# A change at two seams of an FNO, convolution and column-recurrence kernel: where the tile pools lie, the order and queue of the last stores, and who normalises the first columns

## The chip, the cores and the metric

The kernel runs on one core of one Trainium2 chip, as a single program. The metric is its time on the device in microseconds (us), the median over several executions; smaller is better. "The profile" is one further execution, recorded by the hardware profiler: it gives the start and duration of the instructions on each engine, what each waited for, and the traffic of the DMA queues. In its lines PE is TensorE (matmul), DVE VectorE, ACT ScalarE, POOL GpSimd and SP SyncE, which only issues DMAs here. "L733" is line 733 of the kernel before.

## What is computed

The input x has 8 images of 32 channels and 256 x 256 points, in float32. It goes through four layers, each with a group norm (16 groups of two channels) ahead of it and a residual sum behind it:

```python
# layer 0: 32 x 32 modes at either end of the rows are mixed over channels
x = x + _L0_conv_ref(_gn(x), w1r, w1i, w2r, w2i, bias)   # rfft2, einsum, irfft2
# layer 1: the same 5 x 5 kernel on every channel, padding 2
x = x + _L1_conv_ref(_gn(x), kernel, 1, 2)
# layer 2: a gated cell that walks over the columns
x = x + _L2_conv_ref(_gn(x), weight_ih, bias_ih, weight_hh, bias_hh)
# layer 3: running maxima in four directions, then a 1 x 1 convolution
x = x + _L3_conv_ref(_gn(x), W, b)

def _cell(prev_col, cur_col, weight_ih, bias_ih, weight_hh, bias_hh):
    C = cur_col.shape[-1]
    pad = jnp.pad(prev_col, ((0, 0), (1, 1), (0, 0)))
    x = jnp.concatenate([pad[:, :-2], pad[:, 1:-1], pad[:, 2:]], axis=-1)
    i_vals = jnp.einsum('bhk,ok->bho', x, weight_ih) + bias_ih
    h_vals = jnp.einsum('bhc,oc->bho', cur_col, weight_hh) + bias_hh
    ...
    r = jax.nn.sigmoid(r_i + r_h)
    z = jax.nn.sigmoid(z_i + z_h)
    n = jnp.tanh(n_i + r * n_h)
    return n * z + cur_col * (1.0 - z)
```

In layer 2 the first column of the image is the first state; every later column needs the new column to its left and its own normalised values. This makes 255 dependent steps.

## The kernel before

The kernel has four stages, one after another, joined by scratch tensors in DRAM.

**Forward transform and mixing** (`forward_and_mix`, L75). The wanted modes are computed with matmuls and mixed over channels; the mixed modes go from the tiles `sm` to the DRAM tensor `smd`, through the DMA queues of SP and ACT.

**Inverse transform and 5 x 5 convolution** (`inverse_and_conv`, L297). The work runs over 16 units: image b and half h of its channels. Each unit has two parts `ch` of 8 channels. A unit loads its piece of the input into the six buffers `xb` (L379, on GpSimd's DMA queue), and the spectra of its image into `spec` (`load_spectrum`: one DMA of 8-KB rows, two of rows of 128 bytes; the first two images on SP's queue, later ones on ACT's). TensorE forms the inverse transform and the convolution; VectorE adds the residuals (L520) and leaves x1, the input of layer 2, in one of five buffers of 18 KB per partition. The image's 256 columns lie on the partitions in blocks of 28, with 9 tiles for the blocks (`NT = 9`; the last block has tile 0). `squares2` (L525, on ScalarE) takes the sums for the next group norm.

`store(u, ch)` (L534) writes a finished x1 to the DRAM tensor `x2d`, laid out by column: for each quarter `a` of the image's rows it issues three DMAs, the middle blocks, the head (columns 0 to 29, from the tile of block 1) and the tail (the last block). All go through SP's queue; only in the very last store do the odd quarters go through ScalarE's. Behind that store stands the stage's last statement, a fence. In front of it are `statistics(15)` (four small matmuls, four VectorE operations and a `pow` on GpSimd, L569) and `keep` (L572), which puts the last statistics into `stb`.

Columns 0 to 7 of the first seven images are fetched for the recurrence while the last unit is still computed, into the tile `first` (on GpSimd's queue, at the end of the loop over units).

**Column recurrence** (`recurrence`, L684). `turned` (L707) is the transpose of the statistics; from it comes `shift` (L711), the additive term of the normalisation. Eight tiles `hs`, two halves of the batch times four, hold the last states, with one border column at each side of the 64 points; all of every tile is set to zero (L715). Blocks of 8 columns are loaded as `xw` through SP's queue, one DMA for each image (`load`, L720); block 0 is `first`, whose eighth image is loaded here. `normalise` (L731) is one ScalarE operation over 4 columns of one image: tile `xn`. Before the first column all 16 of block 0 are issued.

A step (L807) is one column for one half of the batch (x = 0 or 1); n = 2w + x counts them. In each, the order on the engines is written out by hand:

- TensorE: the matmuls of the gates r, z and n on the old state (`gates`, L786), with the products of the next half step's own column mixed in (`own`, L777).
- ScalarE: sigmoid of r (L828), twice of z (L830 and the next), tanh (L835), then the `normalise` for the next block.
- VectorE: `n = (nh + b) * r` (L829), plus `ni` (L834), then one "piece" of side work (such as the running maximum, L864), times z (L840), plus `a` (L842, the new state in `hs`).
- GpSimd: `a = (1 - z) * x` (L837) and the residual sum of the column (L843), which reads the new state.

ScalarE's sigmoid belongs to another table of functions than the ones that it used before; the load of it stands as ACT_TABLE_LOAD ahead of the first sigmoid.

**Maxima and 1 x 1 convolution** (`maxima_and_mix`, L909).

Inside a stage the order of the instructions on each engine is the order of the program (`manual_schedule`). Each stage opens its own SBUF pools with a `with` block, and they lie one behind another in the order in which they are opened. In `inverse_and_conv` they are, at L314 to L318:

```python
one = ctx.enter_context(tc.tile_pool(name="a2c", bufs=1))   # bias, junk, junk2, five x1
xp = ctx.enter_context(tc.tile_pool(name="a2x", bufs=1))    # spec, xb
wk = ctx.enter_context(tc.tile_pool(name="a2w", bufs=2))    # tt
sm = ctx.enter_context(tc.tile_pool(name="a2s", bufs=3))
```

and in `recurrence` in the same way `one` (turned, shift, hs, bst), `blk` (xw, xn and the running maxima fm), `wk`. The memory of a closed pool is used again by the stage that follows, and the framework adds the waits which that needs. `stb` and `first` have a pool of their own, open over both stages.

Of the kernel before, what the change touches and what calls it, by code (L numbers as in the profile page):

```python
# [10 lines left out]
AF = mybir.ActivationFunctionType  # L11
ALU = mybir.AluOpType
# [5 lines left out]
B, C, H, W = 8, 32, 256, 256  # L18
# [5 lines left out]
A = 4  # L24
Q = H // A


NT = 9
TS = 28
# [263 lines left out]
def columns(x2d, b, lo, hi):  # L293
    return x2d[b, lo:hi].rearrange("w a c q -> (a c) w q")


def inverse_and_conv(tc, k, d, smd, xmean, x2d, stb, first):  # L297
# [6 lines left out]
    nc = tc.nc  # L304
# [6 lines left out]

    PLACES = (1, 2, 3, 5, 6, 7, 8)
    with ExitStack() as ctx:
        one = ctx.enter_context(tc.tile_pool(name="a2c", bufs=1))  # L314
        xp = ctx.enter_context(tc.tile_pool(name="a2x", bufs=1))
        wk = ctx.enter_context(tc.tile_pool(name="a2w", bufs=2))
        sm = ctx.enter_context(tc.tile_pool(name="a2s", bufs=3))
        ps = ctx.enter_context(tc.tile_pool(name="a2p", bufs=1, space=PSUM))  # L318

# [2 lines left out]
        junk = one.tile([P, 16, Q], F32, name="junk")  # L322
# [112 lines left out]
        def squares(u, ch, n, lo, hi, vector=False):  # L435

            for g in range(G):
                x, total = pair_of(u, ch, g, lo, hi), state[u]["sq"][:, ch, g, n : n + 1]
                if vector:
                    nc.vector.scalar_tensor_tensor(  # L440
                        junk2[:, : 2 * (hi - lo)], x, 1.0, x, ALU.mult, ALU.mult, accum_out=total
                    )
                else:
                    nc.scalar.activation(junk[:, : 2 * (hi - lo)], x, AF.Square, accum_out=total)
# [89 lines left out]
        def store(u, ch):  # L534
            b, h = units[u]
            c0 = 2 * CH * h + CH * ch
            x1, to = x1_of(u, ch), x2d[b, :, :, c0 : c0 + CH].rearrange("w a c q -> w a (c q)")
            for a in range(A):
                r = 32 * a
                queue = nc.scalar if a % 2 and 2 * u + ch == 2 * n - 1 else nc.sync  # L540
                queue.dma_start(
                    out=to[TS + 2 : TS * (NT - 1) + 2, a].rearrange("(t w) n -> w t n", w=TS),
                    in_=x1[r + 2 : r + 30, 2:NT].rearrange("w t c q -> w t (c q)"),
                )
                queue.dma_start(out=to[0 : TS + 2, a], in_=x1[r : r + 30, 1].rearrange("w c q -> w (c q)"))
                queue.dma_start(
                    out=to[TS * (NT - 1) + 2 : W, a], in_=x1[r + 2 : r + 32, 0].rearrange("w c q -> w (c q)")
                )

        def statistics(u):  # L550
            b, h = units[u]
# [20 lines left out]
        def keep(u, st):  # L572
            b, h = units[u]
            for kind in range(2):
                nc.vector.tensor_copy(
                    by_pair(stb[:, kind, b, 2 * CH * h : 2 * CH * (h + 1)]), twice(st[:, kind], 2)
                )
# [15 lines left out]
        with tc.manual_schedule(engines=None):  # L593
            load_spectrum(0)
            load_spectrum(1)
            for i in range(3):
                load(0, i)
            spectrum(0)
            for u in range(2):
                begin(u)  # L600
            for c in range(0, CH, 2):
                over_rows(0, c, *(("st", 1), ("up", 3))[c // 2 % 2])
            for p in range(NT):
                transform(0, p)
                if p % 2:
                    over_rows(1, p - 1)
                if p == 4:
                    for ch in range(2):
                        squares(0, ch, 1, 1, 5)
            for ch in range(2):  # L610
                squares(0, ch, 2, 5, NT, ch == 1)
            scale(0, 1, 3)
            transform(1, 0)
            for u in range(n):
                more, beyond = u + 1 < n, u + 2 < n
                for g in range(2 * G):
                    between = []
                    if g == 0 and u == 0:
                        between.append(lambda: scale(u, 0, 3))
                    if g == 3 and more:  # L620
                        between.append(lambda: transform(u + 1, 4))
                    conv(u, g // G, g % G, between)
                    if g < len(PLACES) and more:
                        transform(u + 1, PLACES[g])
                    if g == 2 * G - 1 and beyond:
                        transform(u + 2, 0)
                    if g == 2 * G - 1 and more:
                        scale(u + 1, 0, 3)
                    if g == 1 and u > 0:
                        scale(u, 1)  # L630
                    if g == 2:
                        if u > 0:
                            st = statistics(u - 1)
                        elif beyond:
                            spectrum(units[u + 2][0])
                    if g == G - 1 and beyond:
                        begin(u + 2)
                    if G - 1 <= g < 2 * G - 1 and beyond:
                        over_rows(u + 2, 2 * (g - G + 1))
                    if g == 6 and more:  # L640
                        squares(u + 1, 0, 2, 8, NT)
                    squares2(u, g // G, g % G)
                    if g == 1 and more:
                        for ch in range(2):
                            squares(u + 1, ch, 0, 0, 1)
                    if g == 3 and u > 0:
                        keep(u - 1, st)
                    if g == 5 and more:
                        squares(u + 1, 0, 1, 1, 8)
                    if u % 2 and u + 3 < n:  # L650
                        if g == 2:
                            load_spectrum(units[u + 3][0])
                        elif g == 7:
                            spectrum(units[u + 3][0])
                    if g % G == G - 1 and (u, g) != (n - 1, 2 * G - 1):
                        store(u, g // G)
                    if u == n - 1 and g == G:
                        for b in range(B - 1):
                            nc.gpsimd.dma_start(out=first[:, b], in_=columns(x2d, b, 0, 8))
                if more:  # L660
                    squares(u + 1, 1, 1, 1, NT)
            keep(n - 1, statistics(n - 1))
            store(n - 1, 1)
            tc.declare_fence(nc.tensor.drain().ins, group="conv")

# [18 lines left out]
def recurrence(tc, k, d, x2d, x3d, fwd, stb, first, loaded, mean1, mv3):  # L684
# [10 lines left out]
    with ExitStack() as ctx:  # L695
# [16 lines left out]

        hs = [[one.tile([P, BC, Q + 2], F32, name=f"hs_{x}_{i}") for i in range(NH)] for x in range(NC)]
        for t in hs[0] + hs[1]:
            nc.vector.memset(t, 0.0)  # L715
        bst = one.tile([P, B, NB, 6], F32, name="bst")

        raws, norms, psums = {}, {}, {}
# [1 line left out]
        def load(bi):  # L720
            if bi:
                t = blk.tile([P, B, WB, Q], F32, name=f"xw_{bi}", tag="xw", bufs=4)
                for b in range(B):
                    nc.sync.dma_start(out=t[:, b], in_=columns(x2d, b, bi * WB, (bi + 1) * WB))
            else:
                t = first
                nc.sync.dma_start(out=t[:, B - 1], in_=columns(x2d, B - 1, 0, 8))
            raws[bi] = t
            norms[bi] = blk.tile([P, B, WB, Q], F32, name=f"xn_{bi}", tag="xn")

        def normalise(bi, b, half):  # L731
            w = slice(half * WB // 2, (half + 1) * WB // 2)
            nc.scalar.activation(  # L733
                norms[bi][:, b, w], raws[bi][:, b, w], AF.Identity, bias=shift[:, b : b + 1], scale=sc[:, 1, b : b + 1]
            )
# [142 lines left out]
        with tc.manual_schedule(engines=None):  # L878
            load(0)
            load(1)  # L880
            for half in range(2):
                for b in range(B):
                    normalise(0, b, half)
            for bi in range(NB):
                for wi in range(WB):
                    if wi == WB // 2 and bi + 2 < NB:
                        load(bi + 2)
                    for x in range(NC):
                        step(bi * WB + wi, x)
                        if bi + 1 < NB:  # L890
                            half, b = divmod(NC * wi + x, B)
                            normalise(bi + 1, b, half)
                    running(bi, wi)
                finish(bi)
            tc.declare_fence(nc.tensor.drain().ins, group="signals")
            for piece in pieces[0] + pieces[1]:
                piece()
# [302 lines left out]
```

## Time and profile before

The median of 3 runs is 3101.18 us (3096.61 to 3104.53). The profiled execution took 3099.62 us, of which its span, the time from the first instruction to the last, is 3097.8 us.

Busy time of the engines by stage, in us, as the trace gives it for six windows of the span (PEclk is the granted TensorE clock as a share of full speed; DMA the mean busy share of the 16 DMA engines):

| window | what runs there | length | PE | VectorE | ScalarE | GpSimd | PEclk | DMA |
|---|---|---|---|---|---|---|---|---|
| 0 to 300 | forward, mixing | 300 | 246.4 | 164.5 | 106.6 | 28.9 | 0.85 | 0.86 |
| 300 to 325 | first seam | 25 | 2.0 | 1.7 | 0.0 | 3.3 | 0.50 | 0.99 |
| 325 to 1053 | inverse, convolution | 728 | 705.1 | 557.4 | 481.3 | 117.1 | 0.99 | 0.68 |
| 1053 to 1081 | second seam | 28 | 10.4 | 7.4 | 14.0 | 3.7 | 0.63 | 0.88 |
| 1081 to 2433 | recurrence | 1352 | 1346.0 | 1222.2 | 1111.8 | 700.1 | 1.00 | 0.61 |
| 2433 to 3098 | maxima, 1 x 1 | 665 | 518.1 | 631.1 | 154.9 | 6.8 | 0.90 | 0.82 |
| all | | 3098 | 2827.9 | 2584.2 | 1868.6 | 859.9 | 0.95 | |

A row is read against its length: where an engine's busy time comes near it, that engine has no slack there. In the two seams no compute engine is near its window, and the DMA engines are busy. The granted clock over the whole span is 0.954. Among the largest single groups of instructions of the recurrence, the normalisation (xn from xw) has 496 instructions of 586 ns on ScalarE, and the sum of L843 496 of 685 ns on GpSimd.

### The profile page before, as it was taken

To read this page: it belongs to the slowest core of one execution; us is meant where nothing else is said; L and a number is where in the kernel's file an instruction comes from. 1 tells how busy PE (TensorE), PEld (TensorE's weight loads), DVE (VectorE), ACT (ScalarE), POOL (GpSimd) and SP (SyncE) were. 2 spreads that over 40 slices of the span, in tenths; PEclk is the share of its full clock that TensorE was granted. 3 is DMA by queue.
4 is the path that set the end of the run, shared out by engine and by line. 5 is a ranking of instruction groups with operands and counts; after the bars stand their busy time and mean duration, and the time that the engine had idled before them with its cause. 6 is when DMAs were issued, how large, how long until landed. Compare 5 with 4: busy or idle time off the path is not lost.

```text
span 3097.8 us, 111686 instructions
## 1 busy us (share of the span) xinstructions
PE 2827.9 (91%) x47736; PEld 1625.9 (52%) x47736; DVE 2584.2 (83%) x5178; ACT 1868.6 (60%) x4482; POOL 859.9 (28%) x1247
## 2 busy tenths in 40 slices
PE   7986799999999699999999999999999588888887
PEld 4656244444444366666666666666666333333333
DVE  5753577777777589999999999999999799999997
ACT  3332376667667678888888888888888222222222
POOL 0110011111111255555555555555555300000000
PEclk9985899999999899999999999999999799998998
DMA  9976577777775736656666656666664688888885
GB/s 385 389 278 210 161 226 213 211 210 219 210 215 175 179 91 160 165 143 143 143 150 165 161 142 143 144 155 165 152 146 115 192 319 328 330 322 328 326 327 228
DMA packets 468193, 655.69 MB, mean 212 GB/s; under 512 B 328784, under 2 KB 329696, under 8 KB 441456
## 3 DMA queue, kind: packets, MB, share of 16 engines
q1 hardware_dynamic: 407528, 487.89, 54.1%
q0 software_dynamic: 16784, 84.11, 8.2%
q10 hardware_dynamic: 43384, 76.55, 6.9%
q8 instruction: 374, 6.13, 0.8%
q14 instruction: 123, 1.01, 0.1%
HBM read 371.63 MB, written 272.63 MB: 208 GB/s over the span
## 4 chain that ended last, share of the span: by engine, by line
PE 71%; DVE 20%; DMA 3%; issue 3%; ACT 1%; SPq 0%; POOL 0%; ACTq 0%; DVEq 0%; POOLq 0%
PE vp L487 14%; PE r L753 14%; PE z L753 13%; PE ni L753 6%; PE nh L753 6%; PE up L418 4%; DVE rv L1012 4%; PE yp L131 3%; DVE dq L1018 2%; DVE uq L1020 2%; DVE m L1026 2%; DVE m L1022 2%; DVE m L1024 2%; PE tp L401 2%; PE o L1043 2%
## 5 line engine op out<-in xcount | busy, mean ns | idle before, releaser
L761 PE MATMUL z<-hs,weights 64*64 64x256 f32 x4080 | 539.3, 382 | 0.0
L761 PE MATMUL r<-hs,weights 64*64 64x256 f32 x4080 | 525.0, 375 | 0.0
L761 PE MATMUL ni<-hs,weights 64*64 64x256 f32 x4080 | 524.9, 375 | 0.0
L843 POOL TENSOR_TENSOR xw<-xw,hs 128x256 f32<-128x256 f32 x496 | 339.5, 685 | 635.6 <-DVE hs L842 635.6
L487 PE MATMUL vp<-x,c_conv 64*64 64x512 f32 (+5 forms) x4608 | 460.6, 495 | 4.3 <-DVE x L520 4.3
L1058 ACT ACTIVATE ot<-o,bres 128x512 f32<-128x512 f32 x256 | 154.9, 688 | 505.4 <-PE o L1043 490.0
L520 DVE SCALAR_TENSOR_TENSOR x<-vp,r,x 128x128 f32<-128x128 f32 (+2 forms) x640 | 350.4, 562 | 125.6 <-PE vp L487 106.7
L837 POOL TENSOR_TENSOR a<-zm,xn 128x256 f32<-128x256 f32 x510 | 372.4, 730 | 6.3 <-ACT zm L830 6.1
L835 ACT ACTIVATE n<-n,bih 128x256 f32<-128x256 f32 x510 | 259.2, 508 | 186.3 <-DVE n L834 186.3
L1043 PE MATMUL o<-m,wsc 32*32 32x512 f32 x3072 | 228.6, 724 | 108.1 <-DVE m L1026 104.5
L753 PE MATMUL r<-hs,weights 64*64 64x256 f32 x2040 | 319.1, 389 | 5.0 <-DVE hs L842 4.1
L487 PEld LDWEIGHTS vp<-x,c_conv 64*64 64x64 f32 x4608 | 201.9, 133 | 227.7 <-issue 107.1
L753 PE MATMUL z<-xn,weights 64*64 64x256 f32 x2040 | 305.5, 376 | 14.4 <-ACT xn L733 14.4
L753 PE MATMUL r<-xn,weights 64*64 64x256 f32 x2040 | 305.5, 376 | 1.2 <-ACT rs L828 1.2
L753 PE MATMUL nh<-xn,weights 64*64 64x256 f32 x2040 | 305.7, 377 | 0.0
L753 PE MATMUL z<-hs,weights 64*64 64x256 f32 x2040 | 305.2, 376 | 0.0
L753 PE MATMUL ni<-hs,weights 64*64 64x256 f32 x2040 | 305.2, 376 | 0.0
L733 ACT ACTIVATE xn<-xw,shift,turned 128x256 f32<-128x256 f32 x496 | 290.6, 586 | 0.0
L761 PEld LDWEIGHTS ni<-hs,weights 64*64 64x64 f32 x4080 | 284.5, 133 | 0.3
L829 DVE SCALAR_TENSOR_TENSOR n<-nh,bhh,rs 128x256 f32<-128x256 f32 x510 | 246.3, 483 | 45.9 <-ACT rs L828 31.4
L761 PEld LDWEIGHTS r<-hs,weights 64*64 64x64 f32 x4080 | 280.9, 131 | 0.2
L828 ACT ACTIVATE rs<-r,brz 128x256 f32<-128x256 f32 x510 | 241.3, 473 | 53.9 <-PE r L761 32.5
(162 smaller groups left out, 6233.8 us busy)
## 6 DMA issues: line engine op xcount, KB each, us to landing
xb<-in_xl_dram POOLq DMA_DIRECT2D x96, 768.0 KB, 6.3
xa<-in_xt_dram SPq DMA_DIRECT2D x64, 1024.0 KB
x<-x3d SPq DMA_DIRECT2D x32, 2048.0 KB
fw<-fwd SPq DMA_DIRECT2D x32, 2048.0 KB
out_dram<-ot ACTq DMA_DIRECT2D x64, 1024.0 KB
xw<-x2d SPq DMA_DIRECT2D x248, 256.0 KB
fwd<-fm SPq DMA_DIRECT2D x248, 256.0 KB
x3d<-xw SPq DMA_DIRECT2D x248, 256.0 KB
```

Of the source, the lines that this page charges most:

```text
L487: ins = nc.tensor.matmul(vps[bank][to, :, dst], lhsT=k.conv[r, P : P + 64] if kind == 2 else k.conv[r, o], rhs=pair_of(u, ch, g, lo, hi, s ...
L520: nc.vector.scalar_tensor_tensor(x, src[o], r1[rows, g : g + 1], x, ALU.mult, ALU.add, accum_out=s1[rows, 0, n, ch, g : g + 1])
L733: nc.scalar.activation(norms[bi][:, b, w], raws[bi][:, b, w], AF.Identity, bias=shift[:, b : b + 1], scale=sc[:, 1, b : b + 1])
L753: ins = nc.tensor.matmul(out[r], lhsT=weights[r, kind, gate, :], rhs=src[r], start=start, stop=stop)
L761: ins = nc.tensor.matmul(out[pairs[1 - i]], lhsT=weights[r, kind, gate, :], rhs=prev[r, :, q0 : q0 + Q], start=False, stop=stop,)
L828: rs = nc.scalar.activation(r, p["r"], AF.Sigmoid, bias=brz[:, 0:1])
L829: nc.vector.scalar_tensor_tensor(m, p["nh"], bhh[:, 2:3], r, ALU.add, ALU.mult)
L835: nc.scalar.activation(m, m, AF.Tanh, bias=bih[:, 2:3])
L837: product = nc.gpsimd.tensor_tensor(a, zm, cur, ALU.mult)
L843: nc.gpsimd.tensor_tensor(raw, raw, new, ALU.add)
L1043: nc.tensor.matmul(pts[b2][i][32 * j : 32 * j + 32].rearrange("p (w q) -> p w q", q=Q), lhsT=wsc[q, b2, t, :], rhs=src[j][q, b2], start=first,
L1058: nc.scalar.activation(ot[:, i], pts[b2][i], AF.Identity, bias=bres[:, b2, i : i + 1])
```

## The change

It has seven parts.

1. In `inverse_and_conv` the pools xp and wk are opened before `one`, so that `spec`, `xb` and `tt` lie at lower addresses than bias, junk and the five x1.
2. In `store` the head of a quarter is issued before its middle and tail, for every unit. In the last store the DMAs are sorted by part, so that the four heads come first, then the four middles, then the four tails; and all of them go through SP's queue.
3. A sigmoid of one element per partition, with its result thrown into `junk`, is put on ScalarE ahead of the last statistics.
4. Of the tiles `hs` only the two border columns are set to zero.
5. The eighth image of `first` is loaded through GpSimd's queue, not SP's.
6. Before the first column only the first half of block 0 (columns 0 to 3) is normalised on ScalarE, eight operations.
7. The other half, eight operations, is done on VectorE as `tensor_scalar` (multiply, then add), two behind each half step of columns 1 and 2.

```diff
--- before.py
+++ after.py
@@ -311,9 +311,9 @@
 
     PLACES = (1, 2, 3, 5, 6, 7, 8)
     with ExitStack() as ctx:
-        one = ctx.enter_context(tc.tile_pool(name="a2c", bufs=1))
         xp = ctx.enter_context(tc.tile_pool(name="a2x", bufs=1))
         wk = ctx.enter_context(tc.tile_pool(name="a2w", bufs=2))
+        one = ctx.enter_context(tc.tile_pool(name="a2c", bufs=1))
         sm = ctx.enter_context(tc.tile_pool(name="a2s", bufs=3))
         ps = ctx.enter_context(tc.tile_pool(name="a2p", bufs=1, space=PSUM))
 
@@ -535,17 +535,21 @@
             b, h = units[u]
             c0 = 2 * CH * h + CH * ch
             x1, to = x1_of(u, ch), x2d[b, :, :, c0 : c0 + CH].rearrange("w a c q -> w a (c q)")
-            for a in range(A):
-                r = 32 * a
-                queue = nc.scalar if a % 2 and 2 * u + ch == 2 * n - 1 else nc.sync
-                queue.dma_start(
-                    out=to[TS + 2 : TS * (NT - 1) + 2, a].rearrange("(t w) n -> w t n", w=TS),
-                    in_=x1[r + 2 : r + 30, 2:NT].rearrange("w t c q -> w t (c q)"),
-                )
-                queue.dma_start(out=to[0 : TS + 2, a], in_=x1[r : r + 30, 1].rearrange("w c q -> w (c q)"))
-                queue.dma_start(
-                    out=to[TS * (NT - 1) + 2 : W, a], in_=x1[r + 2 : r + 32, 0].rearrange("w c q -> w (c q)")
-                )
+            last = 2 * u + ch == 2 * n - 1
+            parts = [(a, part) for a in range(A) for part in range(3)]
+            for a, part in sorted(parts, key=lambda x: x[1]) if last else parts:
+                r, queue = 32 * a, nc.sync
+                if part == 0:
+                    queue.dma_start(out=to[0 : TS + 2, a], in_=x1[r : r + 30, 1].rearrange("w c q -> w (c q)"))
+                elif part == 1:
+                    queue.dma_start(
+                        out=to[TS + 2 : TS * (NT - 1) + 2, a].rearrange("(t w) n -> w t n", w=TS),
+                        in_=x1[r + 2 : r + 30, 2:NT].rearrange("w t c q -> w t (c q)"),
+                    )
+                else:
+                    queue.dma_start(
+                        out=to[TS * (NT - 1) + 2 : W, a], in_=x1[r + 2 : r + 32, 0].rearrange("w c q -> w (c q)")
+                    )
 
         def statistics(u):
             b, h = units[u]
@@ -659,6 +663,7 @@
                             nc.gpsimd.dma_start(out=first[:, b], in_=columns(x2d, b, 0, 8))
                 if more:
                     squares(u + 1, 1, 1, 1, NT)
+            nc.scalar.activation(junk[:, 0, 0:1], k.mhalf[:, 0:1], AF.Sigmoid)
             keep(n - 1, statistics(n - 1))
             store(n - 1, 1)
             tc.declare_fence(nc.tensor.drain().ins, group="conv")
@@ -712,7 +717,7 @@
 
         hs = [[one.tile([P, BC, Q + 2], F32, name=f"hs_{x}_{i}") for i in range(NH)] for x in range(NC)]
         for t in hs[0] + hs[1]:
-            nc.vector.memset(t, 0.0)
+            nc.vector.memset(t[:, :, 0 : Q + 2 : Q + 1], 0.0)
         bst = one.tile([P, B, NB, 6], F32, name="bst")
 
         raws, norms, psums = {}, {}, {}
@@ -724,12 +729,17 @@
                     nc.sync.dma_start(out=t[:, b], in_=columns(x2d, b, bi * WB, (bi + 1) * WB))
             else:
                 t = first
-                nc.sync.dma_start(out=t[:, B - 1], in_=columns(x2d, B - 1, 0, 8))
+                nc.gpsimd.dma_start(out=t[:, B - 1], in_=columns(x2d, B - 1, 0, 8))
             raws[bi] = t
             norms[bi] = blk.tile([P, B, WB, Q], F32, name=f"xn_{bi}", tag="xn")
 
-        def normalise(bi, b, half):
+        def normalise(bi, b, half, vector=False):
             w = slice(half * WB // 2, (half + 1) * WB // 2)
+            if vector:
+                nc.vector.tensor_scalar(
+                    norms[bi][:, b, w], raws[bi][:, b, w], sc[:, 1, b : b + 1], shift[:, b : b + 1], ALU.mult, ALU.add
+                )
+                return
             nc.scalar.activation(
                 norms[bi][:, b, w], raws[bi][:, b, w], AF.Identity, bias=shift[:, b : b + 1], scale=sc[:, 1, b : b + 1]
             )
@@ -878,15 +888,17 @@
         with tc.manual_schedule(engines=None):
             load(0)
             load(1)
-            for half in range(2):
-                for b in range(B):
-                    normalise(0, b, half)
+            for b in range(B):
+                normalise(0, b, 0)
             for bi in range(NB):
                 for wi in range(WB):
                     if wi == WB // 2 and bi + 2 < NB:
                         load(bi + 2)
                     for x in range(NC):
                         step(bi * WB + wi, x)
+                        if bi == 0 and 1 <= wi < 3:
+                            for b in range(4 * wi + 2 * x - 4, 4 * wi + 2 * x - 2):
+                                normalise(0, b, 1, True)
                         if bi + 1 < NB:
                             half, b = divmod(NC * wi + x, B)
                             normalise(bi + 1, b, half)
```

## Prediction

> **What bounds the kernel now.** I read the page's chain first: TensorE holds 71% of it, in stages that the change doesn't touch. So I went to the two seams at which the diff acts, asking there for the chain in order of time, then for the timeline of single engines.
>
> The seam into the recurrence, chain of waits:
>
> ```profile
> 1053.22 0.65 ACT junk L527
> ...
> 1062.51 3.17 DMA x2d<-x
> 1066.09 0.98 DVE turned L707
> 1067.08 0.28 DVE hs L715
> 1067.61 7.95 ACT xn L733 x16
> 1075.57 0.43 issue
> 1075.99 0.59 ACT xn L733
> 1076.60 1.28 ACT L828
> 1077.89 0.48 ACT rs L828
> 1078.40 0.50 DVE n L829
> ...
> 1081.00 0.43 PE r L753 x2
> ```
>
> Convolution work ends at 1053.1; the last store of x1 lands at 1065.67 (semaphore updates); then transpose, 16 normalises, two of the next block, the table load and the first sigmoid follow one another. Only at 1081.0 is TensorE in its stride. The seam lasts 28 us; that is all that this part of the change can draw on.
>
> The stride after it, timeline of VectorE:
>
> ```profile
> 1088.84 0.48 DVE L829 SCALAR_TENSOR_TENSOR n<-nh,bhh,rs 128x256 f32<-128x256 f32 x1 [0.17 <-ACT rs L828]
> ...
> 1090.59 0.41 DVE L840 TENSOR_TENSOR n<-n,zs 128x256 f32<-128x256 f32 x1
> 1091.04 0.42 DVE L842 TENSOR_TENSOR hs<-n,a 128x256 f32<-128x256 f32 x1
> 1091.43 0.48 DVE L829 SCALAR_TENSOR_TENSOR n<-nh,bhh,rs 128x256 f32<-128x256 f32 x1
> ...
> 1094.11 0.48 DVE L829 SCALAR_TENSOR_TENSOR n<-nh,bhh,rs 128x256 f32<-128x256 f32 x1
> ```
>
> A column takes 5.27 us (1088.84 to 1094.11). Between L842 of the first half and L829 of the second VectorE has no gap, and 0.17 us before the next column: what is put there is late at once.
>
> The seam before it, from the mode products into the inverse transform; chain, then timeline of GpSimd:
>
> ```profile
> 292.37 3.31 PE mp L269 x58
> ...
> 297.45 3.50 DMA smd<-sm
> ...
> 302.41 19.21 DMA spec<-smd
> ...
> 323.59 5.33 PE tp L401 x32
> ```
>
> ```profile
> 302.18 3.16 POOL L379 DMA_DIRECT2D xb<-in_xl_dram  x6 [86.32 <-issue]
> ```
>
> The pools are swapped here too. TensorE is done at 295.7 and waits until 323.6 for the spectra, which share the DMA engines with six loads of 768 KB.
>
> **What the skill says.** "DMA: Bandwidth & Descriptors", Queues, rings and completion order: a DMA engine goes round robin between queues, a packet at a time. The trace agrees: from 306 to 317 it has some 64 packets of 6 KB and 70 of 128 B per us, so the spectra's last rows (4096 of 128 B) wait for the loads of x, and then run at about 1300 per us. "SBUF — State Buffer", Who interferes with whom: a 2-port VectorE op, such as tensor_scalar, and a GpSimd op exclude each other. Nothing in this trace has just that pair; L864 at 0.72 us beside an idle GpSimd and 0.90 beside a busy one shows a milder form. "ScalarE: Activation LUTs", What ACT_TABLE_LOAD costs: 1283 ns; the trace has 1.28.
>
> **How far a reused buffer waits.** This decides the most. Before, "turned" (3 KB at the start of its pool) lies on bias and junk, which no late DMA reads, and yet waits 7.9 us for the stores of x1. The first xb buffer lies on weights alone, and yet its load starts only after smd<-sm has landed (300.95). So a new pool waits for everything in each old pool that it touches. By the sizes in the code (bytes per partition): the inverse stage's "one" has 98,432, its xp 53,248, wk 16,384; in the recurrence "one" has 19,744 and blk 131,072. With xp first, the recurrence's "one" touches xp alone. blk, which has xn and xw, reaches from 19,744 to 150,816 and still touches the pool of x1 from 69,632 on. So transpose, shift and hs are freed from the stores; the first normalise and the xw loads aren't.
>
> **The change part by part** (against the profiled execution: 3099.62 us, span 3097.8, 1.8 outside).
>
> 1. *Stores on SP alone, heads first.* ACT loses six DMA issues; SP gets them. The four heads (30 rows each, 120 of 1024) need only the tile of column block 1, finished by 1050.8, so they can leave before 1053.1. For the other 904 rows SP needs, by the unit before (12 issues from 1018.84 to 1030.85, 11.7 ns a row), 10.6 us: to 1063.7; landing 1.6 after the last issue, as there: 1065.3. At 10.9 ns, as in an earlier unit, 1064.5. I take 1065.0, against 1065.67: 0.7 gained. Two queues had brought nothing, since SP's second half waited at 1060.4 for a semaphore of ACT's.
> 2. *Transpose and the rest early; memset on 8 elements (L948 has 65 ns for such a one) instead of 264 (0.278).* All done by 1060, behind the stores. The first normalise comes 0.3 after the landing, not 1.94: 1065.3 instead of 1067.61, 2.3 gained with part 1. Their cover is the stores; without it they cost some 2 us again.
> 3. *first[7] on POOL.* Behind the pow (to 1058.0), 0.9 to issue, 4 to 9 us to land as its seven sisters had (3.8 to 8.8): at most 1068, needed at 1068.8. Costs nothing. SP goes straight to the xw loads: the first lands 3.5 later as before, 1069, and ScalarE comes to it at 1065.3+8x0.497 = 1069.3. Just in time.
> 4. *Eight normalises fewer, table load ahead.* ScalarE would be free 8x0.497+1.28 = 5.3 sooner. But the sigmoid needs r: TensorE starts 2.13 after the first normalise, partly at half clock, and ends r 7.87 after it (1075.48). So the sigmoid moves from 10.28 after the first normalise to 7.92, L829 to 8.43: 1073.7, not 1078.40. 2.4 more gained. The table load itself falls at 1054.3 in idle time; without that it costs 1.28. Identity already runs within sigmoid's table.
> 5. *Eight tensor_scalar on VectorE, two behind each half step of columns 1 and 2.* L201 (128x1024) takes 0.70: 0.53 at two elements per cycle and 0.17 fixed; so 128x256 is 0.30 (estimate). A pair D is 0.6 if free; up to 1.98 if each first waits for a GpSimd sum (L843, 0.69), which starts at just that point. Bounds 0.4 (overlapping) and 2.0; I take 0.75, since GpSimd has one sum there. Behind them stands L829, with ScalarE's tanh and TensorE's next column behind that. By the stride above a column then takes 5.10+2D instead of 5.27: at 0.75 it is 6.60. L829 of column 3: 1073.7+10.20+4x0.75 = 1086.9, against 1088.84. Three quarters of parts 1, 2 and 4 go back. The end of this seam gains 1.9; nothing later catches up or loses, as the stride is a closed loop.
> 6. *The seam before.* xp now touches only xf and the first weights, so the six xb loads wait for TensorE alone: issue at 296.2, first packets 1.15 later as at 334.65, 297.4, instead of 305.3. For 12.9 us they hold the engines, and the last two smd stores (1024 packets of 256 B each, from 298.0 on) get one packet for one of x: 46 of 64 on an engine by 310.4, the rest by 311.4. The bias load, now on the sm buffers too, stands ahead of the spectra on SP: 0.4. Spectra from 312.1: 1.3 to the first packet, 2.3 for the 8 KB rows, 3.1 for the fine ones, 0.5: 319.3, against 321.6. Gain 2.3. If x comes later than 299.5 the stores escape, and the spectra end at 316: 5.6. If arbitration is rougher, 322.5: -0.9.
> 7. *The order of the other stores.* Same queue, same rows: nothing; five x1 buffers cover it.
>
> Sum: 1.9+2.3 = 4.2. Own time 3095.4; the median lies 1.56 above that execution: 3097.0.
>
> **Rivals.** (a) *As summed:* 3097.0. (b) *The smd stores escape.* For it: GpSimd took 3.1 us, not 1.15, from issue to first packet at 302.18. Against it: the engines were then full of 8 KB rows. 5.6+1.9 = 7.5: 3093.7. (c) *Waits go tile by tile.* xn and the first xw then lie off x1, and normalising starts on the heads at about 1060.0 instead of 1065.3: 5.3 more, less about 1 for xw loads that queue behind the stores: 4.2+4.3 = 8.5, with escape 12: 3090. Against it: the two waits above. (d) *VectorE's pairs make it slower.* Place: behind L842 of columns 1 and 2; price 4D. The gain of parts 1, 2 and 4 is then 4.9, so the seam loses from D = 1.2, and the whole from D = 1.8. At the bound 2.0 it is -3.1+2.3: 0.8 slower, 3102. For it: GpSimd's sum starts when the pair does. Against it: a half step has one sum, and both operations of a pair would have to lose. (e) *Nothing arrives:* the loads of x merely change places with the stores and the pairs eat the seam: 3100.5.
>
> **How the numbers follow.** Chances: (a) 0.5, (b) 0.15, (c) 0.12, (d) 0.08, (e) 0.15. I predict (a), 3097.0. Its own range, from D between 0.5 and 1.3 and the seam before between -0.9 and 2.3, is 3095 to 3102. The three runs before lie between 3096.6 and 3104.5, so about 0.3% (9.3 us) is what can be told from no change. The range 3089 to 3103 takes in (b), most of (c) and (d), and some scatter. Faster by over 0.3% (under 3091.9) is most of (c) and the scatter of (b) and (a): 0.2; slower (over 3110.5) no case reaches without scatter: 0.05; within: 0.75.
>
> **What would show it.** Transpose at 1058 to 1060 less the earlier seam's gain, with the first normalise still ending a wait for DMA x2d<-x; eight normalises, two of the next block, no table load before the sigmoid; tensor_scalar near 0.3 us and four half steps of about 3.3 us; tp 2 us earlier, xb issued at 296. If the first normalise starts while stores still fly, (c) is right; if smd<-sm lands before 304, (b); if tensor_scalar shows 0.9 or more, (d). I would be wrong altogether if the stride, 5.27 us over 255 columns, changed: 0.04 us there makes 10.

## The result

The changed kernel took a median of 3095.75 us in 8 runs (3093.82 to 3107.23), the kernel before 3103.86 us in 8 (3096.61 to 3106.54): ratio 0.9983, 95% interval [0.9969, 0.9997]. A second comparison, 14 runs against 27, gave 0.9994 [0.9985, 1.0004]. The forecast, 3097.0, is near the first median. Its reasons are another matter. Seven of the experiments below were executed once (3092.81 to 3107.41 us, about as far apart as runs of one kernel); they are read from the intervals in their traces, not from these times.

The profiled span fell from 3097.8 to 3091.9 us, by 5.9. To see where, the span is cut at events that both kernels have: the end of the mixing (the last matmul into mp), the first tp (the first matmul of the inverse transform), the end of the convolution (last L520), the first normalise, and L829 (L839 in the changed kernel) of half steps n = 2, 6 and 8. Each column gives the time since the event of the column before it, the last one the time from the end of the convolution to half step 8, in us, from the traces. The rows below the second are the experiments that follow:

| kernel | mixing end, at | to tp | to conv end | to first normalise | to n=2 | n=2 to 6 | conv end to n=8 |
|---|---|---|---|---|---|---|---|
| before | 295.66 | 27.92 | 729.54 | 14.49 | 10.79 | 10.44 | 40.98 |
| changed | 292.12 | 28.44 | 729.45 | 12.87 | 7.65 | 13.90 | 39.60 |
| before, again | 295.94 | 28.05 | 729.31 | 14.54 | 10.78 | 10.45 | 41.03 |
| changed, again | 294.99 | 28.23 | 736.58 | 12.74 | 8.20 | 13.89 | 40.01 |
| pools only | 295.95 | 28.18 | 731.37 | 12.98 | 10.78 | 10.76 | 39.78 |
| no pairs | 293.92 | 28.04 | 736.14 | 12.79 | 9.35 | 10.45 | 37.85 |
| eighth image on SP | 295.14 | 28.32 | 737.31 | 11.50 | 8.92 | 13.90 | 39.50 |
| pairs early | 295.46 | 28.21 | 729.72 | 12.83 | 7.65 | 10.80 | 36.54 |
| xn apart | 294.61 | 28.43 | 729.61 | 6.39 | 9.20 | 13.91 | 34.69 |
| x behind | 296.14 | 17.02 | 737.94 | 12.84 | 7.70 | 13.91 | 39.63 |
| old order of stores | 294.15 | 28.34 | 730.60 | 12.84 | 7.83 | 14.20 | 40.04 |
| swap back | 295.79 | 28.59 | 735.77 | 14.25 | 8.49 | 13.90 | 41.83 |
| all | 292.79 | 17.25 | 734.33 | 5.97 | 8.26 | 10.45 | 29.93 |

From the first two rows: the first seam is 0.5 us longer, not 2.3 shorter; the second is 1.4 shorter, not 1.9. That is 0.9 us. Of the other 5.0 us, 3.5 arose before the mixing ended and 1.5 in the last stage (L829 of half step 510 to the end of the last L1058, L1070 in the changed kernel, 664.37 against 662.83; the expectation below counts 6.4 less), where both kernels run the same instructions. Behind half step 8 the recurrence runs at the old pace (n=8 to 20: 31.72 and 31.73).

The second seam of the changed kernel, chain of waits (start, us, what):

```profile
1050.85 1.67 SPq L545
...
1059.45 3.09 DMA x2d<-x
1062.88 2.08 ACT xn L743 x4
1065.00 1.12 PE z L763 x4
...
1070.02 0.48 ACT rs L838
1070.53 0.49 DVE n L839
...
1072.65 0.42 DVE hs L852
1073.07 1.02 DVE xn L739 x2
1074.09 0.41 DVE n L839
```

The first normalise still ends a wait for the stores of x1, as forecast; the table load has gone from the chain. Each pair of VectorE normalises stands in it whole, between the new state and the next L839.

The first seam, chain of waits, and the loads of x in GpSimd's timeline:

```profile
288.82 3.25 PE mp L269 x112
...
293.61 15.29 DMA smd<-sm
...
310.73 7.96 DMA spec<-smd
...
320.56 5.33 PE tp L401 x32
```

```profile
292.70 3.21 POOL L379 DMA_DIRECT2D xb<-in_xl_dram  x6 [78.79 <-PE mp L269]
```

The loads of x now wait for TensorE alone, as worked out, and start ahead of the last stores of the modes, which take 15.29 us instead of 3.50. The wait for "spec" has become a wait for "smd".

### The profile page after: what moved, and what is told of

It reads as the page before. It is cut to its first block, busy times and chain, and to the rows that moved or that the text cites. A ratio compares the mean times of both kernels' runs of the same rounds, so it can differ in the third digit from the quotient of the medians.

```text
span 3091.9 us, 111713 instructions
## 1 busy us (share of the span) xinstructions
PE 2823.9 (91%) x47736; PEld 1623.0 (52%) x47736; DVE 2587.1 (84%) x5186; ACT 1866.0 (60%) x4475; POOL 862.4 (28%) x1248
## 4 chain that ended last, share of the span: by engine, by line
PE 66%; DVE 20%; issue 3%; DMA 2%; ACT 1%; SPq 1%; POOL 0%; DVEq 0%; ACTq 0%; POOLq 0%
PE vp L487 14%; PE r L763 14%; PE z L763 13%; PE ni L763 6%; PE nh L763 6%; PE up L418 4%; DVE rv L1024 4%; DVE dq L1030 2%; DVE uq L1032 2%; DVE m L1038 2%; DVE m L1036 2%; DVE m L1034 2%; PE tp L401 2%; PE o L1055 2%; PE mp L269 2%
## 5 line engine op out<-in xcount | busy, mean ns | idle before, releaser
L1070 ACT ACTIVATE ot<-o,bres 128x512 f32<-128x512 f32 x256 | 155.1, 688 | 503.6 <-PE o L1055 433.0
L520 DVE SCALAR_TENSOR_TENSOR x<-vp,r,x 128x128 f32<-128x128 f32 (+2 forms) x640 | 350.7, 563 | 124.9 <-PE vp L487 106.0
L839 DVE SCALAR_TENSOR_TENSOR n<-nh,bhh,rs 128x256 f32<-128x256 f32 x510 | 246.3, 483 | 41.7 <-ACT rs L838 28.2
```

The lines of the kernel that those rows point to most:

```text
L520: nc.vector.scalar_tensor_tensor(x, src[o], r1[rows, g : g + 1], x, ALU.mult, ALU.add, accum_out=s1[rows, 0, n, ch, g : g + 1])
L839: nc.vector.scalar_tensor_tensor(m, p["nh"], bhh[:, 2:3], r, ALU.add, ALU.mult)
L1070: nc.scalar.activation(ot[:, i], pts[b2][i], AF.Identity, bias=bres[:, b2, i : i + 1])
```

## The experiments

**Both kernels again.**

> The kernel before, once more. My theory (T): the profiled pair differs by 5.9 us, but only -0.9 of it is the change (first seam +0.5, second seam -1.4); -3.5 arose in the forward stage and -1.5 in the maxima, which the change doesn't touch, and is scatter. So here the end of the mixing may lie anywhere from 291 to 297 us, while mixing end to first tp stays at 27.9 +- 0.5 and the end of the convolution to L829 of half step 8 at 41.0 +- 0.4. Rival (R): the forward stage and the maxima are faster because of the change: then the mixing ends at 295.7 +- 0.5 again, and n510 to the last output takes 658.0.

> The changed kernel, once more. T: mixing end to first tp 28.4 +- 0.5, end of the convolution to half step 8 39.6 +- 0.4; the end of the mixing scatters as in the kernel before, and the ratio of the times is 0.9995 to 0.9985. R: the mixing ends at 292.1 +- 0.5 again and the ratio stays near 0.9975.

Before: 3100.18 us (13 runs, 3097.56 to 3106.1). Changed: 3098.04 (14 runs, 3094.34 to 3107.52), 0.9994 as given above. The intervals at the seams repeat to 0.1 in the kernel before and 0.4 in the changed one; the gain at the second seam is 1.4 us in the first pair of profiles and 1.0 in the second. The mixing's end lay at 295.9 and 295.0, so that of the 3.5 us 0.9 were left, and in the profiles of the changed kernel and its variants it lies anywhere between 292.1 and 296.1. Of the last stage's 1.5 nothing was left (664.24 and 664.64). Neither is a property of the change, and the rival R falls. The changed kernel's second profile shows something else, 7.0 us more in the convolution; see the last section.

**The pool order alone.**

```diff
-        one = ctx.enter_context(tc.tile_pool(name="a2c", bufs=1))
         xp = ctx.enter_context(tc.tile_pool(name="a2x", bufs=1))
         wk = ctx.enter_context(tc.tile_pool(name="a2w", bufs=2))
+        one = ctx.enter_context(tc.tile_pool(name="a2c", bufs=1))
```

> The kernel before with the order of the pools alone. T: the six loads of x start about 2 us before the mixing's last result is stored, the stores of the modes land 16 to 17 us after the mixing's end instead of 5.3, and first tp comes at 28.4 +- 0.6 after it: no gain. As predicted it would be 25.6. At the second seam the transpose no longer waits for the stores of x1, so the first normalise comes 12.9 after the end of the convolution instead of 14.5; all else there as before, L829 of half step 2 10.8 after the first normalise: 39.4 to half step 8.

Measured 28.18 and 12.98, as expected; to half step 8 39.78. What I had not expected is 1.8 us more in the convolution. VectorE's timeline shows its origin:

```profile
1014.96 1.28 DVE L427 TENSOR_TENSOR x<-up,xb 128x512 f32<-128x512 f32 x2
1016.37 2.25 DVE L715 MEMSET hs<- 128x264 f32 x8
1018.54 0.23 DVE L520 SCALAR_TENSOR_TENSOR x<-vp,r,x 128x128 f32<-128x128 f32 x1
```

Freed from the stores of x1, the memsets of hs ran in the middle of the convolution, ahead of an L520 of the 15th of the 16 units, and from there on it was 1.7 us behind the kernel before. In the changed kernel the same eight, on 8 elements each, take 0.17 there, and its convolution is as long as before (729.45 against 729.54). So the pool order alone gained 1.5 at the first normalise and gave 1.8 back; to pay it needs the small memsets.

**All sixteen normalises on ScalarE again** (the rest as changed).

```diff
-            for b in range(B):
-                normalise(0, b, 0)
+            for half in range(2):
+                for b in range(B):
+                    normalise(0, b, half)
...
-                        if bi == 0 and 1 <= wi < 3:
-                            for b in range(4 * wi + 2 * x - 4, 4 * wi + 2 * x - 2):
-                                normalise(0, b, 1, True)
```

> The changed kernel with all 16 normalises of the first block on ScalarE again, ahead of the loop. T: the eight on VectorE cost more (3.46 us between half steps 2 and 6) than the eight on ScalarE, which TensorE's first gates mostly cover: the first sigmoid comes 18 x 0.497 = 8.95 after the first normalise instead of 7.14, L829 at 9.5 instead of 7.65, and half steps 2 to 6 take 10.4 instead of 13.9. Net 1.6 us less: 38.0 from the end of the convolution to half step 8, against 39.6. Rival: ScalarE's eight are not covered and cost 4 us: 40.2.

37.85, as expected: VectorE's share, where the change put it, costs 1.75 us more than it saves (2.2 against the changed kernel's second profile). (This profile's convolution lost 6.6 us at unit 8 in a wait for a store of x1, which the comparison within the seam leaves out.)

**The eighth image on SP's queue again.**

```diff
-                nc.gpsimd.dma_start(out=t[:, B - 1], in_=columns(x2d, B - 1, 0, 8))
+                nc.sync.dma_start(out=t[:, B - 1], in_=columns(x2d, B - 1, 0, 8))
```

> The changed kernel with the eighth image of the first columns on SP's queue again, behind the stores. T: on GpSimd's queue it moved beside the last stores (packets of 4 KB from 1056 to 1061) and cost them 0.6 us, which is why the stores landed 12.5 us after the end of the convolution and not 11.9 as predicted. Here the first normalise comes 12.2 after the end of the convolution instead of 12.8, and the eighth image still lands before ScalarE reaches it, 3.5 us later: end of the convolution to half step 8 is 39.1 to 39.5. Rival: the stores are bound by their own packets of 2 KB on one queue: first normalise at 12.8 as in the changed kernel, and the eighth image, now behind them, delays the second half batch: 40 or more.

The first normalise came at 11.50, earlier than I expected: on GpSimd's queue this load costs the stores 1.3 us. But the next stretch grew by 1.27, from 7.65 to 8.92, and the sum is the same, 39.50. The rival blames the late image for that; ScalarE's timeline speaks against it:

```profile
1072.27 4.04 ACT L743 ACTIVATE xn<-first,shift,turned 128x256 f32<-128x256 f32 x8 [8.85 <-DMA x2d<-x]
1080.68 0.47 ACT L838 ACTIVATE rs<-r,brz 128x256 f32<-128x256 f32 x1 [3.39 <-PE r L771]
```

All eight normalises follow one another without a wait, in 4.04 us as in the changed kernel. Late is TensorE, for which the first sigmoid waits. From its first gate matmul (2.13 us after the first normalise in both) to that sigmoid, in the changed kernel, then here (window, its length, busy time and instructions of PE, PEld, DVE, ACT and POOL, granted clock, DMA share, GB/s):

```profile
1065.01:1070.02 5.01, 4.92 (x52) 2.74 (x56) 0.56 (x2) 2.89 (x6) 1.35 (x2) 0.70 1.19 269
1074.40:1080.68 6.28, 6.19 (x52) 3.31 (x56) 0.57 (x2) 2.89 (x6) 1.36 (x2) 0.56 1.23 279
```

The same 52 matmuls take 5.01 us at a mean granted clock of 0.70 and 6.28 at 0.56; length times clock is 3.51 and 3.52. The whole 1.27 is the clock's. Whether the change of queue delayed the clock, or this execution alone, one profile doesn't tell; if it was this execution alone, SP's queue would be 1.3 us better.

**VectorE's normalises ahead of the first step.**

```diff
             if w == 0:
+                for b in (range(0, 3), range(3, 6))[x]:
+                    normalise(0, b, 1, True)
                 nc.vector.tensor_copy(new, cur)
+                for b in range(6 * x, 8 * x):
+                    normalise(0, b, 1, True)
...
-                        if bi == 0 and 1 <= wi < 3:
-                            for b in range(4 * wi + 2 * x - 4, 4 * wi + 2 * x - 2):
-                                normalise(0, b, 1, True)
```

> The changed kernel with the eight VectorE normalises ahead of the first step, beside ScalarE's eight, where VectorE is idle (three before the copy of each half batch's first column, two behind). T: a pair costs its whole 1.02 us behind L842 because the loop is closed there; in the idle time it costs nothing. L829 of half step 2 at 7.65 after the first normalise as before, half steps 2 to 6 in 10.45 instead of 13.9, end of the convolution to half step 8 36.1 to 36.6. Rival: beside GpSimd's first sums VectorE's operations take longer and hold up the copies: half step 2 comes 1 us or more later. If each takes 0.30 us here instead of 0.55, GpSimd slowed them in the changed kernel; if 0.55, it did not.

36.54, 3.06 less than with the pairs in the loop; half steps 2 to 6 took 10.80, 0.35 over what was expected. VectorE's timeline:

```profile
1066.30 1.06 DVE L739 TENSOR_SCALAR xn<-first,turned,shift 128x256 f32<-128x256 f32 x3 [6.56 <-DMA x2d<-x]
1068.32 0.29 DVE L825 COPY hs<-xn 128x256 f32<-128x256 f32 x1 [0.97 <-ACT xn L743]
1068.53 1.42 DVE L739 TENSOR_SCALAR xn<-first,turned,shift 128x256 f32<-128x256 f32 x3
1070.29 0.29 DVE L825 COPY hs<-xn 128x256 f32<-128x256 f32 x1 [0.34 <-ACT xn L743]
1070.50 1.10 DVE L739 TENSOR_SCALAR xn<-first,turned,shift 128x256 f32<-128x256 f32 x2
```

Three take 1.06 us while GpSimd is idle and 1.42 while it forms its first sum (1068.76 to 1069.48). In groups, one takes 409 ns in the first case and 594 in the last, which lies beside the second sum; 592 in the changed kernel's loop. The prediction took from the Trainium skill ("SBUF — State Buffer", Who interferes with whom) that the two operations exclude each other; measured is a slowing, with both at work at once. GpSimd pays too: its sum takes 0.79 us beside a pair, 0.68 without.

**xn in a pool of its own.**

```diff
+        xnp = ctx.enter_context(tc.tile_pool(name="bx", bufs=2))
         blk = ctx.enter_context(tc.tile_pool(name="bb", bufs=2))
...
-            norms[bi] = blk.tile([P, B, WB, Q], F32, name=f"xn_{bi}", tag="xn")
+            norms[bi] = xnp.tile([P, B, WB, Q], F32, name=f"xn_{bi}", tag="xn")
...
                             half, b = divmod(NC * wi + x, B)
-                            normalise(bi + 1, b, half)
+                            todo.append((bi + 1, b, half))
+                        if todo and (bi or NC * wi + x >= 4):
+                            normalise(*todo.pop(0))
```

> The changed kernel with the tiles xn in a pool of their own ahead of blk, so that they lie over xp alone (19.7 to 52.5 KB), and with the normalises of later blocks four half steps later, so that ScalarE doesn't stand waiting for block 1. T: a pool waits for all of each pool that it touches; xn touched the pool of x1 before, and doesn't now. The first normalise starts with shift, 6.5 us after the end of the convolution instead of 12.8, while the stores of x1 still fly; the eighth image (landed 11.8 after) ends the last of the eight; half step 2 comes 6 us sooner: 33.4 to 34.0 from the end of the convolution to half step 8. Rival: the loads, not the pool, hold the first normalise: 39 or more.

ScalarE's timeline:

```profile
1059.04 3.55 ACT L744 ACTIVATE xn<-first,shift,turned 128x256 f32<-128x256 f32 x7 [3.74 <-DVE shift L717]
1064.32 0.60 ACT L744 ACTIVATE xn<-first,shift,turned 128x256 f32<-128x256 f32 x1 [1.74 <-DMA first<-x2d]
1067.73 0.47 ACT L839 ACTIVATE rs<-r,brz 128x256 f32<-128x256 f32 x1 [2.81 <-DMA xw<-x2d]
```

The first normalise starts behind shift, 6.39 after the convolution, while stores still fly: the wait belonged to the pool, not to the data. The eighth image is now late, by 1.74. Yet 34.69 came out instead of 33.4 to 34.0 because of the clock again, as the same window, first gate matmul to first sigmoid, shows:

```profile
1061.16:1067.74 6.58, 6.49 (x52) 3.48 (x56) 0.57 (x2) 2.03 (x5) 1.36 (x2) 0.54 0.51 133
```

Length times clock is 3.55, so that at most 0.1 us is left for the late image; whether it delayed the clock stays open.

**x behind the spectra.**

```diff
             load_spectrum(0)
-            load_spectrum(1)
             for i in range(3):
                 load(0, i)
+            load_spectrum(1)
...
-                nc.gpsimd.dma_start(
+                (nc.gpsimd if u else nc.sync).dma_start(
```

> The changed kernel with the first unit's six loads of x on SP's queue behind the spectra of image 0 (and those of image 1 behind them). T: the first seam is a matter of the order in which the same bytes pass the DMA engines: stores of the modes alone land 5.3 us after the mixing, the spectra 9.5 later, first tp 16.5 to 18 after the mixing's end instead of 28.2; x's first piece lands 4 to 5 us behind the spectra, before VectorE asks for it 7 us after tp, so tp to the end of the convolution stays at 729.5. Gain 10 to 11 us. Rival: VectorE then waits for x, and what tp gains is lost at L427: tp to the end of the convolution grows by 8 or more.

The chain of waits:

```profile
289.95 6.20 PE mp L269 x197
...
297.92 3.49 DMA smd<-sm
...
303.32 7.96 DMA spec<-smd
...
313.15 6.18 PE tp L401 x32
```

The stores take 3.49 us again, the spectra 7.96 as in the changed kernel, and tp comes 17.02 after the mixing. VectorE's wait ahead of the first L427, put down to TensorE and not to x, grew from 7.1 to 8.0 us only. In this profile the convolution was 8.5 longer all the same than in the changed kernel: 7.1 of it at unit 8, as in "no pairs", far from the first loads; so the time of the run, 3095.02, shows only a part of the gain.

**The old order in the other stores.**

```diff
-            for a, part in sorted(parts, key=lambda x: x[1]) if last else parts:
+            for a, part in sorted(parts, key=lambda x: x[1]) if last else [(a, part) for a in range(A) for part in (1, 0, 2)]:
```

> The changed kernel with the old order of parts (middle, head, tail) in every store but the last. T: with heads first a store begins 2.2 us sooner and meets the fine rows of the spectra that ScalarE's queue loads for unit 8; in two of seven profiles that load then took 20 us instead of 8, SP stood 10 us behind it, and the convolution lost 6.6 to 7 us. Here the load takes 7 to 10 us in the profile, and fewer of the runs lie above 3103 us (7 of 22 did with heads first): 0 to 3 of 14; the median 1 us lower. Rival: the slow executions come from TensorE's clock and from chance alone, and as many lie above 3103. At the seams as the changed kernel: 28.2 and 39.6.

A miss: as many long runs as the rival had it. 8 of 22 lay above 3103 us, no fewer than the 7 of 22 of the changed kernel, and 9 of 27 of the kernel before in the same comparison; the median was 3099.14, ratio 0.9994 [0.9985, 1.0003]. The long load itself is real, as SP's waits show for "no pairs" from 680 to 716 us (what waited, for what, us in total, times, longest):

```profile
SPq L545 <- DMA spec<-smd: 9.8, 1, 9.8
```

and VectorE's timeline behind it:

```profile
715.50 0.69 DVE L427 TENSOR_TENSOR x<-up,xb 128x512 f32<-128x512 f32 x1 [4.35 <-DMA x2d<-x]
```

It occurred in 2 of 8 profiles with heads first and in none of 5 with the old order. That may be chance; whether the new order causes it stays open.

**The pools back in the old order** (the rest as changed).

> The changed kernel with the pools in the order of before: all parts but the first. T: the six loads of x wait for the stores of the modes again and first tp comes 27.9 to 28.1 after the mixing's end (28.2 with the swap); at the second seam the transpose waits for the last store of x1 and the first normalise comes 13.8 to 14.2 after the end of the convolution instead of 12.8, so that the end of the convolution to half step 8 takes 40.6 to 41.0. So the swap's whole worth is 0.8 to 1.2 us. Rival: it is worth the 4.6 us that the sum of the prediction gave it at both seams.

28.59 at the first seam, where 27.9 to 28.1 was expected: a little above the swapped kernels (28.04 to 28.44). 14.25 at the first normalise, 1.4 later than with the swap. The total of 41.83 is 0.8 over what was expected, all of it in the stretch to half step 2, and that again is the clock (first gate matmul to first sigmoid 5.86 us at 0.60, which is 3.52). The swap is worth 1.4 us at the first normalise and nothing at the first seam.

**All together.**

> All that the experiments found, together: xn in a pool of its own over xp, later normalises four half steps later, the eight VectorE normalises ahead of the first step, x's first loads behind the spectra, the eighth image fetched right behind the heads and before the last statistics, the old order of parts in all stores but the last. T: mixing end to first tp 17, end of the convolution to half step 8 34.7 - 3.1 - 1.5 = 30.1, tp to the end of the convolution 730.5; 22 us less than before, 21 less than the changed kernel: median 3076 to 3082, ratio 0.9925 to 0.9940. Rival: the gains don't add, since behind the first normalise TensorE's first gates at half clock set the pace: 33 or more, ratio 0.9945 or more.

3083.73 us in 6 runs (3073.37 to 3086.31), ratio 0.9934 [0.9915, 0.9952]; every one of its runs is shorter than any run of the kernel before or of the changed kernel. The seams came as forecast, 17.25 and 29.93. The median lies above the expected range; its profile had 4.8 us more in the convolution, from the clock (below). ScalarE's timeline has no wait for a store or for the eighth image:

```profile
1045.52 1.28 ACT L666 ACT_TABLE_LOAD   x1
...
1050.34 4.04 ACT L744 ACTIVATE xn<-first,shift,turned 128x256 f32<-128x256 f32 x8 [3.32 <-DVE shift L718]
1058.09 0.47 ACT L843 ACTIVATE rs<-r,brz 128x256 f32<-128x256 f32 x1 [3.71 <-PE r L772]
```

## Why the prediction was right or wrong

The direction and the wait that stayed were right. That the time fits is luck: of the 4.2 us forecast the two pairs of profiles show 0.9 and 0.8 at the seams, all at the second, while the medians of one kernel lie up to 3.7 us apart between comparisons (3100.18 to 3103.86 before, 3095.75 and 3098.04 changed). By its steps:

- *How far a reused buffer waits:* right, and the point on which all hung. The pools' sizes gave which waits stay (normalise, xw) and which go (transpose, loads of x). Moving xn by one pool removed the wait that the prediction said would remain.
- *Stores on SP alone, 0.7 gained:* no gain. They landed 12.5 us after the convolution, as before; the step had 11.9. It failed together with the next: with the eighth image back on SP's queue the first normalise came at 11.50, so the stores were at least as early as this step had them.
- *first[7] on POOL "costs nothing":* wrong. Only its own landing was costed, not the engines that it shares with the last stores: without it the first normalise came 1.3 us sooner.
- *Transpose and memsets done behind the stores:* the transpose, yes. The memsets went to the convolution, where at their old size the pool order alone lost 1.8 us.
- *Sigmoid 7.92 after the first normalise:* 7.14 and 7.69 in the two profiles of the changed kernel, up to 8.70 in its variants with the same 52 matmuls. The step took TensorE's time from the row of before, a part of it at half clock; that part changes from execution to execution.
- *A pair at 0.75 us:* 1.02. The estimate of 0.30 for one operation came from a row of another shape; it takes 0.41 beside an idle GpSimd and 0.59 beside its sum. Four pairs lengthened half steps 2 to 6 by 3.46 (13.90 less 10.44), not 3.0. The closed loop, which gives nothing of this back, was right. Rival (d) had the right mechanism: against ScalarE doing all sixteen, the pairs lose 1.75.
- *The seam before, 2.3 gained:* nothing, -0.5 in this pair. The stores of the modes did share the engines with x as described, but two terms were too small. Their first packets came 5.6 us after the mixing's end, not 2.3, and they landed 16.8 after it (293.61 + 15.29 less 292.12) instead of 15.7; the spectra landed 9.8 behind them (310.73 + 7.96) instead of 7.9. The order that helps is the opposite one: x last.

## What to carry to other kernels

When a seam waits for DMAs, write down the order in which the same bytes pass, and put first what the next instruction needs: that was worth 11 us here, where starting a large load early was worth nothing. Work moved out of the way of one engine belongs into idle time of the other, not behind the instruction that closes a loop: the same eight operations cost 3.1 us more in one place than in the other. When a pool is moved, ask of each user what it will now run before: freed instructions may land in the middle of a busy stage.

## What the runs showed of the hardware

TensorE's granted clock differs between executions at the same place; in the traces it is either full or half. At the second seam it is half at first. In the changed kernel and in seven variants with the same first gates it returned to full 3.0 to 6.0 us after the first gate matmul, and length times mean clock from there to the first sigmoid is 3.5 to 3.6 us in every one of them. So the column "to n=2" holds up to 1.5 us of clock (an estimate: half of the 3.0 by which its return differs), as much as the change is worth there.

It also dips inside the convolution. Ahead of L360 TensorE stands idle for 1.4 us in both kernels. In the profile before, the 8 us around one such gap run at full clock; in the changed kernel's second profile the same 8 us, which lie 2 us later there as L360 does (626.51 against 624.56), have 0.79:

```profile
622.00:630.00 8.00, 6.64 (x81) 3.24 (x72) 6.68 (x23) 7.72 (x19) 1.47 (x1) 1.00 0.82 252
```

```profile
624.00:632.00 8.00, 6.64 (x52) 3.23 (x44) 5.10 (x19) 7.72 (x18) 1.47 (x1) 0.79 0.81 252
```

TensorE was busy for as long and got through 52 matmuls instead of 81. Each such dip costs 1.4 to 1.7 us, by the times of L520, and three to five of them made 4.7 to 7.7 us in one execution: more than the change. So it was in 4 of 13 profiles (one dip in two more). The three of the kernel before and of the pools alone have none but one at 446 us, near which several others have theirs; since 9 of 27 runs of the kernel before also lay above 3103 us, I don't put them down to the change, but what sets them off stays open.
